# A planned two-layer kernel (cross attention, then a recurrent layer) on one core: one-bank matmul tiles are allotted to whichever step can begin, under a new table of due times

## Chip, cores and metric

The kernel runs on one core of a Trainium2 chip. The metric is device time in microseconds (us), from the start of the program to its end, and less is better. A core has five engines, each with its own instruction queue that it works through in order: TensorE (PE in the profile; PEld is its weight load), VectorE (DVE), ScalarE (ACT), GpSimd (POOL) and SyncE (SP), which here issues the transfers (DMAs) between the chip's main memory and the on-chip memories. Matmul results land in PSUM, a memory of banks of 128 x 512 numbers in f32; all other on-chip data lie in SBUF.

## The reference

Input: `x` and a context `ctx`, each 32 sequences x 128 tokens x 512 numbers, and a mask. Two layers follow each other; everything is f32.

Layer 0 is cross attention with 32 query heads and 8 key heads of 16 numbers:

```
q = x @ Wq + bq;  k = ctx @ Wk + bk;  v = ctx @ Wv + bv
attn = softmax(q k^T / 4 + mask);  x1 = layernorm((attn v) @ Wo + bo + x) * gamma + beta
```

Layer 1 is a recurrent layer with 32 heads of 16 x 16 state, whose start state comes from `ctx`:

```
xn = ln(x1);  sx = (xn of the token before) - xn
xxx = tanh((xn + sx*maa_x) @ maa_w1) -> five mixes;   x5[i] = xn + sx*(maa_stack[i] + xxx[i] @ maa_w2[i])
w = exp(-exp(time_decay + tanh(x5[1] @ decay_w1) @ decay_w2))
k = x5[0] @ Wk^T;  v = x5[2] @ Wv^T;  r = x5[3] @ Wr^T;  g = silu(x5[4] @ Wg^T)
per token t:  a = k_t v_t^T;  out_t = r_t (u*a + s);  s = a + w_t * s
x2 = x1 + (groupnorm(out) * g) @ Wo^T
xn2 = ln(x2);  xk, xr = xn2 + sx2 * (maa_k, maa_r)
y = x2 + sigmoid(xr @ fWr^T) * (relu(xk @ fWk^T)^2 @ fWv^T)
```

## The kernel before

**Work.** Both layers take the sequences in 16 pairs (`gr`, 256 tokens). Layer 0 (`attend`, L483) runs over all pairs first and leaves its result in main memory (`x1d`). Layer 1 is made of three functions for a pair:

- `front` (L998): the norm of a pair's rows `xt`, transposes on PE (`pxnt`), the shift (`sxt`) and the first mix (`xx`); `ph0` and a tanh give `h0`; `px5` (L1025) are small row-tiled matmuls whose results DVE turns into the five x5 (L1041: index 0 feeds k, 1 the decay, 2 v, 3 r, 4 g), to which POOL adds xn (L1055). Then `pdd` (L1090, column-tiled), and the big matmuls `pk`, `pv`, `pr`, `pg` (L938), each in two blocks (its first and second half of the channels, `_0` and `_2`) of eight matmuls, which the profile records as sixteen; `pew` gives the decay `ew`. v goes to main memory (`vd`, L1105).
- `recurrence` (L1180): four chunks `c` of 128 channels, and in each four values `dd`. v comes back spread over the partitions (`kv`, L1230, 1 MB in eight DMAs for two values of `dd`); ACT puts the start state into its first column (L1243), POOL multiplies it by k (L1252), DVE runs the recurrence as a scan (`a`, L1267) and multiplies by r (`ar`, L1281), and PE sums over the state (`acc`, L1296, column-tiled). `pd`, `own` and `pc` are the term of the token itself and the centring of the norm. `w4` (L1191) is the decay that the scan reads, one buffer.
- `tail` (L1336): `pvar` and `rstd` (an ACT square root, a DVE reciprocal), spread over heads by `pb` (L1357), the gate `gt`, `pwo` (L956), the sum `x1c` on DVE with its norm statistics, transposes `pxnc`, mixes `yk` and `yr`, then `pkk` (L938), `prr`, `pkv` (L956) and the result `rr`. The weights `fk` and `fr` come from main memory for each pair, into one buffer.

**Order.** No scheduler of the compiler decides the order. The kernel's own planner does, a class `Plan` (L152). `add` (L176) records a step: its engine, an assumed duration (`mm`, `dve`, `act`, `pool_`, L299 on), what it reads and writes, and a due time, which is the pair's number plus the entry of the table (`WHEN0` for layer 0, `WHEN1` for layer 1) under the step's engine and name. `give_out` (L238) then walks through an assumed run: on each engine it looks among the steps whose inputs are given out and which are due no more than `ahead` pairs after the earliest step left (SP's are free of that limit), takes the one that can begin soonest or, among those that begin within 0.3 us, the one that is due first, and emits the engine's instruction. So the table and the rule set the order in which instructions stand in each queue, and nothing else; waits between engines come from what is read and written.

**Places.** Tiles come from pools of a fixed number of buffers (`tag`, L168). In PSUM, layer 1 has one `a` (two banks), one `acc` (one bank), `w4` (two banks) and three buffers `g` of one bank each, which hold the result of every other matmul. In SBUF, `kv` has three buffers, `x5` four. `_turns` (L224) numbers the tiles of each tag by due time, and `_places` (L197) gives a step its place: it refuses if a tile's turn hasn't come, and if no buffer is free it takes the one whose last use ends first in the assumed run. The line on turns is the one that is changed:

```python
        if self.turns and any(c.turn - self.begun[c.tag] >= taken[c.tag] for c in fresh):
            return None, gone
```

Layer 0 has `turns` switched off (L425) and its own planner object.

Of the kernel before, what the change touches and what calls it, by code (L numbers as in the profile page):

```python
# [66 lines left out]
}  # L67
WHEN1 = {
    "ACT": """
        att 0: 8.9413, att 1: 10.3245, att 2: 10.9514, att 3: 4.2202, ew 0: 3.0530, ew 1: 7.1294, ew 2: 5.4799,  # L70
        ew 3: -0.1804, gt 0: 2.7896, gt 2: 7.2564, h0: 4.2793, hd: -0.7228, kk 0: 1.5652, kk 2: 8.9401,
        kv 0 0 0: 2.8237, kv 0 0 1: 2.8350, kv 0 1 0: 6.5988, kv 0 1 1: 4.7931, kv 1 0 0: 11.5248, kv 1 0 1: 12.1370,
        kv 1 1 0: 8.1713, kv 1 1 1: 8.4770, kv 2 0 0: 11.3074, kv 2 0 1: 0.7816, kv 2 1 0: 10.6862, kv 2 1 1: 7.1872,
        kv 3 0 0: 19.3264, kv 3 0 1: 5.1004, kv 3 1 0: 5.3317, kv 3 1 1: 6.5296, pk 0: 7.8527, pk 2: 3.7734,
        pv 0: 2.8655, pv 2: 13.4147, r 0: 10.0348, r 2: -0.1824, rr 0: 13.0999, rr 1: 2.8864, rstd: 5.6019,
        sq 0: -0.0986, sq 1: 8.8327, sq 2: 0.5974, sq 3: 5.6588, w4 0: 6.7771, w4 1: 3.1835, w4 2: 6.2518,
        w4 3: 1.3276, xnc 0: 5.1909, xnc 1: 3.5402, xnc 2: 5.5512, xnc 3: 9.4093, xnt 0: 4.3436, xnt 1: 6.3722,
        xnt 2: 7.1367, xnt 3: 8.6670, xx 0: 11.9355, xx 1: 6.5413, xx 2: 5.6875, xx 3: 9.8818, yk 0: 11.1356,
        yk 1: 1.7804, yk 2: 15.8112, yk 3: 13.9956, yr 0: 7.4657, yr 1: 8.8095, yr 2: 3.2938, yr 3: 8.7878,
        zc 0: 7.6581, zc 1: 0.9023, zt 0: 10.9657, zt 1: 5.2637  # L80
    """,
    "DVE": """
        a 0 0: -0.5883, a 0 1: -0.2414, a 0 2: 0.1043, a 0 3: 8.0118, a 1 0: 7.0047, a 1 1: 12.1762, a 1 2: 5.6912,
        a 1 3: 9.0685, a 2 0: 9.3322, a 2 1: 6.5083, a 2 2: 6.9110, a 2 3: 0.9712, a 3 0: 7.3177, a 3 1: 7.6874,
        a 3 2: 2.3097, a 3 3: 12.5406, ar 0 0: 2.4656, ar 0 1: 9.7666, ar 0 2: 5.7906, ar 0 3: 7.9178, ar 1 0: 6.6300,
        ar 1 1: 1.2202, ar 1 2: 6.5895, ar 1 3: 8.7855, ar 2 0: 28.3612, ar 2 1: 16.5392, ar 2 2: 12.3754,
        ar 2 3: 11.7973, ar 3 0: 9.1129, ar 3 1: 12.3189, ar 3 2: 9.0665, ar 3 3: 1.8400, gn 0: 8.4672, gn 1: 5.8193,
        gn 2: 3.6790, gn 3: 6.5194, gt 0: 0.0430, gt 2: -0.3529, own 0: 7.8602, own 1: 10.0300, own 2: 6.6987,
        own 3: 5.2960, pb 0: 0.7953, pb 1: 8.4093, pb 2: 4.1923, pb 3: 8.8563, raw 0: 2.2489, raw 1: 0.4033,
        raw 2: 5.9725, raw 3: 6.8204, rk 0: -0.4021, rk 1: 1.1444, rr 0: 7.1091, rr 1: 5.2378, rstd: 2.3485,  # L90
        st c 0: 6.9368, st c 1: 1.2521, st t 0: 8.7646, st t 1: 7.8543, x1c 0: 1.0294, x1c 1: 6.6954, x5 0 0: 2.9930,
        x5 0 1: 7.2539, x5 0 2: -1.0976, x5 0 3: 11.6924, x5 1 0: 8.4707, x5 1 1: -0.2943, x5 1 2: 10.2532,
        x5 1 3: 6.3221, x5 2 0: -0.6575, x5 2 1: 6.4713, x5 2 2: 12.8297, x5 2 3: 15.9903, x5 3 0: 6.5967,
        x5 3 1: 6.3600, x5 3 2: -0.8402, x5 3 3: -0.6696, x5 4 0: 8.4589, x5 4 1: 12.8956, x5 4 2: -0.4045,
        x5 4 3: 5.3981
    """,
    "PE": """
        acc 0: 13.3710, acc 1: 6.5427, acc 2: 6.5657, acc 3: 5.8187, pb 0: 18.0159, pb 2: 13.4697, pc 0: 0.6934,
        pc 1: 3.6234, pc 2: 5.2455, pc 3: 6.5762, pd 0: 1.0255, pd 1: 5.0703, pd 2: 6.9998, pd 3: 6.9286, pdd: 8.4674,
        pew 0: 6.2963, pew 2: 8.3876, pg 0: 1.2658, pg 2: 11.7555, ph0: 5.5651, pk 0: -0.5984, pk 2: -0.5853,  # L100
        pkk 0: 6.0318, pkk 2: 6.3700, pkv 0: 3.8400, pkv 1: 1.5996, pr 0: 0.4302, pr 2: -0.2452, prr 0: 3.2418,
        prr 1: 6.5661, pv 0: 20.6763, pv 2: -0.4713, pvar: 9.0706, pwo 0: 6.3422, pwo 1: 7.2520, px5 1 0: 6.5332,
        px5 1 2: 4.1685, px5 2 0: 10.0966, px5 2 2: 2.9044, px5 4 0: 2.5948, pxnc 0: 11.8548, pxnc 2: 5.6357,
        pxnt 0: 6.9871, pxnt 2: 5.3933
    """,
    "POOL": """
        kv 0 0 0: 5.5169, kv 0 0 1: 7.8442, kv 0 1 0: 9.0891, kv 0 1 1: 15.0789, kv 1 0 0: 17.4626, kv 1 0 1: 18.1051,
        kv 1 1 0: 6.4738, kv 1 1 1: 2.9970, kv 2 0 0: 11.4247, kv 2 0 1: 9.0041, kv 2 1 0: 5.1827, kv 2 1 1: 4.0282,
        kv 3 0 0: 7.8783, kv 3 0 1: 7.3985, kv 3 1 0: 8.4451, kv 3 1 1: 4.8441, rr 0: 5.3640, rr 1: 1.7889,
        sd c 0: 6.4756, sd c 1: 7.8170, sd t 0: 3.5686, sd t 1: 15.8010, sxc 0: 1.3067, sxc 2: 1.2094, sxt 0: 14.0948,  # L110
        sxt 2: 3.1827, x5 0 0: 6.6556, x5 0 2: 3.8406, x5 1 0: -0.9487, x5 1 2: 5.0243, x5 2 0: 7.7721,
        x5 2 2: 5.1770, x5 3 0: 5.2660, x5 3 2: 5.0072, x5 4 0: 17.6798, x5 4 2: 9.4950, xx 0: 0.3524, xx 2: 3.0003,
        yk 0: 7.2907, yk 2: 13.2242, yr 0: 7.8715, yr 2: 13.9395
    """,
    "SP": """
        fk: 4.3606, fr: 6.4556, kv 0 0 0: 17.3353, kv 0 1 0: 0.8314, kv 1 0 0: 11.4633, kv 1 1 0: 5.2653,
        kv 2 0 0: 13.6957, kv 2 1 0: 2.0768, kv 3 0 0: 0.9291, kv 3 1 0: 16.9878, rr 0: 1.7956, rr 1: 8.0232,
        s0 0: 0.8911, s0 1: 7.1710, vd 0: 4.3598, vd 1: 6.6057, vd 2: 0.4074, vd 3: 6.7184, x1c 0: 3.0367,
        x1c 1: 7.8990, x1t 0: 13.2705, x1t 1: 6.6624
    """,  # L120
}

# [29 lines left out]
class Plan:  # L152

    AFTER = {"PE": 0.25, "DVE": 0.1, "ACT": 0.15, "POOL": 0.12, "SP": 0.0}

    def __init__(self, ctx, tc, when, ahead):
# [38 lines left out]
    def _places(self, s):  # L197


        at, gone, taken = 0.0, [], {}  # L200
        fresh = [c for c in s.fresh if c.t is None]
        for c in fresh:
            taken[c.tag] = taken.get(c.tag, 0) + 1
        if self.turns and any(c.turn - self.begun[c.tag] >= taken[c.tag] for c in fresh):
            return None, gone
        taken = {}
        for c in fresh:
            pool, bufs, live = self.pools[c.tag]
            taken[c.tag] = taken.get(c.tag, 0) + 1
            if len(live) + taken[c.tag] <= bufs:  # L210
                continue
            best = None
            for o in live:
                if o not in gone and all(u.end is not None for _, _, u in o.uses):
                    end = max(u.end for _, _, u in o.uses)
                    if best is None or end < best[0]:
                        best = (end, o)
            if best is None:
                return None, gone
            at = max(at, best[0] + 0.1)  # L220
            gone.append(best[1])
        return at, gone
# [15 lines left out]
    def give_out(self):  # L238
        self.turns and self._turns()
        left = {id(s): len(s.before) for s in self.steps}  # L240
        ready = {e: [] for e in self.AFTER}
        free = {e: 0.0 for e in self.AFTER}
        for s in self.steps:
# [4 lines left out]
        while todo:  # L248
# [3 lines left out]
            for e, ss in ready.items():  # L252
                pick = None
                for s in ss:
# [3 lines left out]
                    for s0 in s.before:  # L258
                        at = max(at, s0.end + (0.0 if s0.eng == e else self.AFTER[s0.eng]))
                    room, _ = self._places(s)  # L260
# [68 lines left out]
def xattn_rwkv_kernel(  # L329
# [53 lines left out]
    x1c = [Cell(None, None, f"x1d_{b}", t=x1d[b]) for b in range(B)]  # L383
# [37 lines left out]
    with ExitStack() as sa:  # L421
        wa = sa.enter_context(tc.tile_pool(name="wa", bufs=1))
        wt = sa.enter_context(tc.tile_pool(name="wt", bufs=3))
        pl = Plan(sa, tc, WHEN0, 15.2739)
# [30 lines left out]
        for i in range(2):  # L455
            t = wa.tile([T, G, 4, 2, 2, S], F32, name=f"v2_{i}")
# [5 lines left out]
        for i in range(4):  # L462
            t = dram.tile([4, 8, T], F32, name=f"rd_{i}")
            rds.append(Cell(None, None, f"rd_{i}", t=t))

        for c in range(KC):
# [13 lines left out]
                r=[pt],  # L480
# [326 lines left out]

    pl = Plan(ctx, tc, WHEN1, 13.2672)  # L810
    fix = ctx.enter_context(tc.tile_pool(name="fix", bufs=1))
    for tag, bufs in (("xt", 2), ("xc", 2), ("s0", 3), ("z", 3), ("xn", 2), ("sx", 2), ("x5", 4), ("h0", 1), ("hd", 1)):
        pl.tag(tag, bufs)
# [11 lines left out]
    kx, vx, vd = [], [], []  # L825
    for i in range(2):
        t = fix.tile([P, KC, G, T], F32, name=f"kx{i}")
        kx.append(Cell(None, None, f"kx{i}", t=t))
        t = fix.tile([P, KC, 1 + N], F32, name=f"vx{i}")
# [3 lines left out]
        for c in range(KC):  # L833
            t = dram.tile([HC, 4, 4, N], F32, name=f"vd{i}_{c}")
# [3 lines left out]
    t = wp.tile([P, 4, G, T], F32, name="w4")  # L838
    for i in range(2):
        nc.vector.memset(t[:, 2 * i : 2 * i + 2], 0.0)  # L840
    w4 = Cell(None, None, "w4", t=t)
# [683 lines left out]
```

## Time and profile before

| | us |
|---|---|
| three runs | 2156.69, 2154.84, 2150.53 (median 2154.84) |
| the profiled execution by its own clock | 2150.95 |
| its span, first to last instruction | 2149.2 |
| PE busy in the span (a weight load beside it: 1305.8) | 1992.6 (93%) |
| DVE / POOL / ACT busy | 1783.0 (83%) / 1294.0 (60%) / 1058.0 (49%) |
| mean clock granted to TensorE | 0.962 |
| first layer-1 load (`x1t`) / first `acc` / last `acc` begin at | 633.7 / 695.8 / 2088.9 |
| moved by DMA | 252.23 MB, mean 117 GB/s |

How to read it: the profile comes from one execution, with every engine's instructions on one time axis. "Busy" is the time in which an engine had an instruction in work; matmuls overlap each other, so a busy PE is not PE at its peak. "Idle before" is the gap ahead of an instruction, with the instruction or DMA that ended it. The granted clock is the share of its full speed at which TensorE was let run. In lines, `px` stands for `px5`, `x` for `x5`, `w` for `w4` and so on: trailing numbers of names are left out.

The costliest single groups of layer 1 are the 256 products on POOL (`kv`, 2349 ns each), the 256 scans on DVE (`a`, 2294 ns) with their 256 products (`ar`, 1217 ns), and on PE the blocks of L938 and L956, about 120 us in all for each of `pk`, `pv`, `pr`, `pg`, `pkk`, `pwo`, `pkv` and `prr`.

### The profile page before, as it was taken

To read this page: it belongs to the slowest core of one execution; us is meant where nothing else is said; L and a number is where in the kernel's file an instruction comes from. 1 tells how busy PE (TensorE), PEld (TensorE's weight loads), DVE (VectorE), ACT (ScalarE), POOL (GpSimd) and SP (SyncE) were. 2 spreads that over 40 slices of the span, in tenths; PEclk is the share of its full clock that TensorE was granted. 3 is DMA by queue.
4 is the path that set the end of the run, shared out by engine and by line. 5 is a ranking of instruction groups with operands and counts; after the bars stand their busy time and mean duration, and the time that the engine had idled before them with its cause. 6 is when DMAs were issued, how large, how long until landed. Compare 5 with 4: busy or idle time off the path is not lost.

```text
span 2149.2 us, 36169 instructions
## 1 busy us (share of the span) xinstructions
PE 1992.6 (93%) x11908; PEld 1305.8 (61%) x11908; DVE 1783.0 (83%) x2182; ACT 1058.0 (49%) x3473; POOL 1294.0 (60%) x1081
## 2 busy tenths in 40 slices
PE   5999999999958779999999999999999999999977
PEld 4666666666626546566675665656657566575643
DVE  3888888888844888989988899898988989888881
ACT  3888888888842233433434434344343443433332
POOL 1273334343345666777777777777777877777552
PEclk9999999999978889999999999999999999999988
DMA  7232221221024687887977978879788797886851
GB/s 207 61 127 66 62 70 60 68 61 60 27 81 80 114 121 114 146 158 122 175 122 138 167 117 168 130 138 163 120 161 134 141 165 117 162 136 115 163 99 59
DMA packets 155883, 252.23 MB, mean 117 GB/s; under 512 B 50512, under 2 KB 97648, under 8 KB 139312
## 3 DMA queue, kind: packets, MB, share of 16 engines
q1 hardware_dynamic: 149232, 240.27, 59.8%
q10 hardware_dynamic: 6464, 9.66, 1.4%
q8 instruction: 94, 1.54, 0.4%
q14 instruction: 93, 0.76, 0.1%
HBM read 224.12 MB, written 25.69 MB: 116 GB/s over the span
## 4 chain that ended last, share of the span: by engine, by line
PE 52%; DVE 7%; ACT 2%; DMA 1%; issue 1%; POOL 0%; SPq 0%; POOLq 0%; DVEq 0%; ACTq 0%
PE pkk L938 5%; PE pwo L956 5%; PE pk L938 5%; PE pv L938 5%; PE pr L938 4%; PE acc L1296 4%; PE pkv L956 4%; PE pg L938 4%; PE prr L956 4%; DVE a L1267 3%; PE pdd L1090 2%; PE px L1025 2%; DVE x L1041 2%; PE pc L1321 1%; PE pew L1162 1%
## 5 line engine op out<-in xcount | busy, mean ns | idle before, releaser
L1252 POOL TENSOR_TENSOR kv<-kv,kx 128x1016 f32<-128x1016 f32 x256 | 597.6, 2349 | 142.9 <-DMA kv<-vd 63.1
L1267 DVE TENSOR_TENSOR_SCAN a<-w,kv 128x1024 f32<-128x1024 f32 x256 | 587.3, 2294 | 29.1 <-ACT w L1191 8.0
L653 ACT ACTIVATE pr<-pr,mx 128x128 f32<-128x128 f32 x1024 | 398.3, 391 | 53.4 <-DVE mx L641 47.0
L1281 DVE TENSOR_TENSOR ar<-a,r 128x1024 f32<-128x1024 f32 x256 | 311.5, 1217 | 4.4
L1055 POOL TENSOR_TENSOR x<-x,xnt 128x512 f32<-128x512 f32 x160 | 187.2, 1181 | 92.1 <-DVE x L1041 79.4
L653 ACT ACTIVATION_READ_ACCUMULATOR pr<-pr,mx 128x1 f32 x1024 | 193.7, 189 | 0.0
L1041 DVE SCALAR_TENSOR_TENSOR x<-px,col,sxt 128x256 f32<-128x256 f32 x320 | 133.9, 473 | 59.5 <-PE pdd L1090 37.2
L629 DVE TENSOR_TENSOR pr<-sc,m 128x1024 f32<-128x1024 f32 x128 | 153.7, 1210 | 32.1 <-PE sc L613 29.0
L665 PE MATMUL ppT<-ident,pr 128*128 128x128 f32 x1024 | 154.3, 281 | 12.1 <-DVE pT L672 4.3
L665 PEld LDWEIGHTS ppT<-ident,pr 128*128 128x128 f32 x1024 | 115.4, 141 | 77.9 <-issue 25.9
L641 DVE TENSOR_REDUCE mx<-pr 128x8 f32<-128x1024 f32 x128 | 155.5, 1215 | 2.7
L1296 PE MATMUL acc<-ar,give 128*32 128x256 f32 x2048 | 142.5, 394 | 12.6 <-DVE ar L1281 12.6
L672 DVE COPY pT<-ppT 128x512 f32<-128x512 f32 x192 | 128.3, 682 | 22.9 <-PE ppT L665 18.2
L397 POOL TENSOR_SCALAR sd_a<-mv_a 128x1 f32<-128x1 f32 x32 | 7.1, 223 | 214.6 <-DVE mv_a L393 214.5
L716 PE MATMUL pw<-wo,oT 128*128 128x512 f32 x256 | 122.3, 610 | 9.8 <-POOL oT L711 8.8
L938 PE MATMUL pkk<-yk,fk 128*128 128x256 f32 x512 | 121.4, 392 | 6.2 <-POOL yk L905 6.2
L956 PE MATMUL pwo<-wo,gt 128*128 128x512 f32 x256 | 122.2, 612 | 5.0 <-ACT xnt L868 2.9
L938 PE MATMUL pr<-x,wr 128*128 128x256 f32 x512 | 122.0, 387 | 3.8 <-DVE x L1041 3.8
L557 PE MATMUL pq<-xT,wq 128*128 128x256 f32 x512 | 122.9, 389 | 0.7 <-ACT xT L512 0.7
L938 PE MATMUL pk<-x,wk 128*128 128x256 f32 x512 | 123.3, 390 | 0.0
L956 PE MATMUL pkv<-fv,kk 128*128 128x512 f32 x256 | 120.3, 603 | 0.0
L938 PE MATMUL pg<-x,wg 128*128 128x256 f32 x512 | 117.6, 383 | 2.9 <-DVE x L1041 2.9
(146 smaller groups left out, 3714.7 us busy)
## 6 DMA issues: line engine op xcount, KB each, us to landing
kv<-vd SPq DMA_DIRECT2D x1024, 128.0 KB
fk<-in_fWkT_dram SPq DMA_DIRECT2D x16, 1024.0 KB
fr<-in_fWrT_dram SPq DMA_DIRECT2D x16, 1024.0 KB
x<-in_x_dram SPq DMA_DIRECT2D x32, 256.0 KB
ct<-in_ctxT_dram SPq DMA_DIRECT2D x32, 256.0 KB
bc<-rd SPq DMA_DIRECT2D x256, 32.0 KB
x1d<-z SPq DMA_DIRECT2D x32, 256.0 KB
x1t<-x1d SPq DMA_DIRECT2D x32, 256.0 KB
```

Source lines behind the costliest of these rows:

```text
L629: lambda b=b, sc=sc, jp=jp, pr=pr: nc.vector.tensor_tensor(pr(), sc()[:, 2 * jp : 2 * jp + 2].rearrange("p j g e s -> p (j g e) s"), ms[b] ...
L641: lambda pr=pr, mx=mx: nc.vector.tensor_reduce(mx(), pr(), AX.X, ALU.max, negate=True),
L653: nc.scalar.activation(pr()[:, 4 * i + h, :], pr()[:, 4 * i + h, :], AF.Exp, bias=mx()[:, 4 * i + h : 4 * i + h + 1], accum_out=sm()[:, h0 ...
L665: nc.tensor.transpose(pt()[:, h, :], pr()[:, 4 * i + h, :], ident)
L938: nc.tensor.matmul(pp()[:, i], (w() if isinstance(w, Cell) else w)[:, kc, (c + i) * P : (c + i + 1) * P], flat(src()[:, kc]), start=(kc == 0),
L956: nc.tensor.matmul(pp(), src()[:, c, b, :], (w() if isinstance(w, Cell) else w)[:, c, :], start=(c == 0), stop=(c == KC - 1),)
L1041: lambda i=i, c=c, pp=pp, half=half: nc.vector.scalar_tensor_tensor(flat(ts[i]()[:, c]), pp()[:, half], col[:, MS0 + i, c : c + 1], flat(s ...
L1055: lambda i=i, c2=c2: nc.gpsimd.tensor_add(ts[i]()[:, c2 : c2 + 2].rearrange("p c b t -> p (c b) t"), ts[i]()[:, c2 : c2 + 2].rearrange("p ...
L1252: lambda c=c, kv=kv, e=e: nc.gpsimd.tensor_tensor(kv()[:, e, :, :, 1:T], kv()[:, e, :, :, 1:T], k()[:, c, :, 0 : T - 1].unsqueeze(1).broad ...
L1267: lambda kv=kv, a=a, e=e: nc.vector.tensor_tensor_scan(a().rearrange("p j b t -> p (j b t)"), w4().rearrange("p j b t -> p (j b t)"), kv() ...
L1281: lambda c=c, a=a, ar=ar: nc.vector.tensor_tensor(ar(), a().rearrange("p j b t -> p j (b t)"), flat(r()[:, c]).unsqueeze(1).broadcast_to([ ...
L1296: nc.tensor.matmul(acc()[32 * j : 32 * j + 32, :N], give[:, d].rearrange("p e h -> p (e h)"), tiles[d]()[:, j], start=(d == 0), stop=(d == 3),
```

## The change

A new class attribute names a tag, `g`, whose tiles have no turns: a step that needs one may take a free buffer as soon as it can begin, whatever is due earlier. All other tags keep their turns. The table `WHEN1` is another one, found by a search under this rule (its entries now reach up to 45 pairs, so that many steps are ordered by what depends on them, since a step is due no later than what follows from it), and `ahead` of layer 1 goes from 13.2672 to 3.9465. Layer 0, the steps themselves, their assumed durations and the number of buffers stay.

```diff
@@ class Plan
+    FREE = ("g",)
     AFTER = {"PE": 0.25, "DVE": 0.1, "ACT": 0.15, "POOL": 0.12, "SP": 0.0}
@@ def _places(self, s):
-        if self.turns and any(c.turn - self.begun[c.tag] >= taken[c.tag] for c in fresh):
+        if self.turns and any(c.tag not in self.FREE and c.turn - self.begun[c.tag] >= taken[c.tag] for c in fresh):
             return None, gone
@@ layer 1
-    pl = Plan(ctx, tc, WHEN1, 13.2672)
+    pl = Plan(ctx, tc, WHEN1, 3.9465)
@@ WHEN1, "PE"
-        acc 0: 13.3710, acc 1: 6.5427, acc 2: 6.5657, acc 3: 5.8187, pb 0: 18.0159, pb 2: 13.4697, pc 0: 0.6934,
...
+        acc 0: 11.6056, acc 1: 19.5265, acc 2: 29.4448, acc 3: 27.8814, pb 0: 8.7430, pb 2: 16.8465, pc 0: 3.6989,
...
```

## The prediction

> **What bounds the kernel now.** First the page's span in 40 slices. Each slice is 53.7 us; the attention layer fills the first eleven, the recurrent layer the rest.
>
> ```profile
> PE   5999999999958779999999999999999999999977
> DVE  3888888888844888989988899898988989888881
> PEclk9999999999978889999999999999999999999988
> ```
>
> From slice 16 to 38 PE is busy throughout and VectorE (DVE) nearly so. The attention layer isn't touched, so only what comes after about 633 us counts. The chain of work that ended last names PE in nearly every piece there, and its pieces repeat: one pair of sequences ("a period") after the other. I cut the recurrent layer at that repeat and asked for busy time by stretch (stretch, length, then busy us and count of PE, weight load, DVE, ACT, POOL, then clock, DMA share, GB/s):
>
> ```profile
> 891.00:978.14 87.14, 84.69 (x473) 55.41 (x473) 79.31 (x90) 35.03 (x77) 65.89 (x51) 1.00 0.83 148
> 978.14:1066.70 88.56, 86.11 (x473) 55.89 (x473) 79.29 (x90) 35.06 (x77) 65.85 (x51) 0.98 0.83 144
> 1066.70:1155.35 88.65, 86.20 (x473) 55.87 (x473) 79.29 (x90) 35.17 (x77) 65.86 (x51) 0.98 0.84 143
> 1865.27:1957.93 92.66, 88.06 (x476) 56.72 (x476) 83.28 (x95) 36.12 (x78) 70.57 (x55) 0.98 0.80 137
> ```
>
> A period is 88.7 us (ten of the twelve I cut lie at 88.6 to 89.1). One, at full clock, is 1.5 us shorter with the same work; one is 4 us longer. DVE alone needs 79.3 us, the DMA engines 0.83 of the time. So PE bounds, and DVE is 9 us behind it.
>
> Where PE isn't working shows in its timeline of one period (start, length, operation; in brackets the wait before it):
>
> ```profile
> 987.22 1.33 PE L1025 MATMUL px<-h,w 32*128 32x256 f32 x8
> 988.47 0.66 PE L860 MATMUL pxnc<-ident,zc 128*128 128x128 f32 x4
> 991.26 0.64 PE L1090 MATMUL pdd<-x,wd 128*32 128x256 f32 x2 [2.13 <-DVE x L1041]
> ...
> 996.13 1.13 PE L1025 MATMUL px<-h,w 32*128 32x256 f32 x8
> ...
> 1053.86 0.70 PE L1357 MATMUL pb<-rstd,back 32*128 32x256 f32 x4
> ...
> 1057.57 1.44 PE L1357 MATMUL pb<-rstd,back 32*128 32x256 f32 x4
> 1059.23 1.98 PE L956 MATMUL pwo<-wo,gt 128*128 128x512 f32 x4 [0.22 <-ACT xnt L868]
> ```
>
> PE waits 2.13 us for DVE's x5 before `pdd`, and the 32 `pdd` matmuls then take 3.4 us. In the one period at clock 1.00 they take 1.9, behind the same wait:
>
> ```profile
> 904.12 0.41 PE L1090 MATMUL pdd<-x,wd 128*32 128x256 f32 x2 [2.13 <-DVE x L1041]
> ```
>
> Record lengths 0.41 against 0.64 us: after this wait the clock drops in 12 of the 13 periods from 891 us on. Beside it, four `pb` take 1.44 us once and 0.70 elsewhere, eight `px` 1.33 and 1.13, and `pwo` waits 0.22: 1.2 us more of waits. So a period is 88.7 - 2.1 - 1.5 - 1.2 = **83.9 us of PE work**.
>
> [...]
>
> **The change, part by part.** No instruction is added or removed; only the order on each engine differs, which the built programs show.
>
> *Wait before `pdd`.* New order on PE: `px5` of x5 1 and 0, half a `pwo`, two `pd`, eight matmuls `pk` (which need x5 0), then `pdd`. x5 0 is now first on DVE and on POOL. Behind the second `px` stand on DVE four x5 (1.6 us) and on POOL one add (1.18), beside 1.7 + 0.9 us of `pwo` and `pd` on PE; x5 1 comes one POOL add later, beside 3.45 us of `pk`. So -2.1, and with it the drop, -1.5. If that cover failed, what comes late is `pk`, by up to the 2.1 again.
>
> *Waits at `pb` and `pwo`.* The four `pb` now stand apart, the transposes `pxnt` far ahead: -1.2. Bounds: 0 to -1.2.
>
> *More changes of matmul kind.* PE's order has 30 changes per period between full-array, row-tiled, column-tiled and transposing matmuls before, 34 after; returns to full array 9 before, 14 after, entries to row tiling 8 and 7. The price is in the chain:
>
> ```profile
> 1009.51 1.00 PE acc L1296 x16
> 1010.51 3.65 PE pv L938 x16
> 1014.16 3.45 PE pkk L938 x16
> ```
>
> Sixteen matmuls take 0.20 us more behind a tiled group. Net 4 x 0.20 = **+0.8** (bounds 0 and 1.2). [...]
>
> *New waits.* Three slots of the one-bank tag now hold what could begin, and some are given back late. From the end of the second `pwo` to the start of the second `pkk`, the latter takes the slot that DVE's first two x5 of index 3 free; the built program has it wait for DVE. DVE's way there starts with the `x1c` of that same `pwo`. Its prices, from the timeline:
>
> ```profile
> 1000.46 2.29 DVE L1267 TENSOR_TENSOR_SCAN a<-w,kv 128x1024 f32<-128x1024 f32 x1
> 1002.78 1.22 DVE L1281 TENSOR_TENSOR ar<-a,r 128x1024 f32<-128x1024 f32 x1
> 1004.09 2.30 DVE L1267 TENSOR_TENSOR_SCAN a<-w,kv 128x1024 f32<-128x1024 f32 x1
> ```
>
> A scan with its product takes 3.65 us start to start. On DVE: five such pairs 18.25, one more product 1.2, `x1c` with its statistics 1.9, five `own` 2.05, one gate 0.6, four x5 1.6: 25.6 us. On PE between the same points: `pd` twice 0.9, `pk` 3.45, `pdd` 1.9, eight transposes 1.15, `pc` 0.6, `acc` 1.0, `pg` 3.65, `px` 1.05, `pkk` 3.65, `acc` 1.0, `pd` 0.6, `pk`, `pc`, `pk` 3.9: 22.85. So PE waits 25.6 - 22.9 = **+2.7**, in two or three pieces (the first `pkk` waits for the gate, the second `pk` for x5 index 2). Bounds: 0, if DVE enters the stretch ahead, and 2.7 + 1.5, if the last piece drops the clock. A wait of 1.31 us late in this trace was followed by matmuls at full speed, 2.13 us by slow ones; the last piece is about 1.4 to 1.8, so I take no drop.
>
> *DMA.* The stores of v and the fetches of kv behind them (SP, in order) move: the second `pv` is now the last matmul block of a period, its stores pass behind two fetches. They issue some 6 us into the next period and their data is multiplied on POOL some 28 us into it, and a fetch takes 10 to 12 us (below), so 0. Bounds 0 and +1, the rest is the slower rival.
>
> *Sum of a period.* 83.9 + 0.8 + 2.7 = 87.4 against 88.7: -1.3, times the 14 periods between the first and the last pair: **-18 us**.
>
> *Start.* `pv` of pair 0, whose stores open the first scan, stands behind both `pk` and four transposes instead of one `pk`: +3.65 + 0.6, less about 1 that DVE saves later: +3 (0 to +6). *End.* The last `prr` waited 1.74 us for its weights; now all of `pkv` (3.4 us more) stands ahead of it: -2 (0 to -4).
>
> Sum against the profiled execution, 2150.95 us by its own clock (span 2149.2 and 1.8 around it): 2150.95 - 18 + 3 - 2 = **2134 us**. The runs shown have the median 2154.84, 0.2% above that execution; less than 0.3% (6.5 us) can't be told from no change here.
>
> **The rivals.**
>
> *The new wait isn't there.* If DVE reaches the stretch with 2.7 us in hand, a period is 84.7 and the time 2150.95 - 14 x 4.0 + 1 = 2096. For it: DVE has 79.3 us of work in 84.7. Against it: its stretch begins with a result of PE that is nowhere else made up.
>
> *The wait comes in one piece, and the clock drops.* 87.4 + 1.5 = 88.9: 2150.95 + 3 + 1 = 2155, no change. For it: 2.13 us does it in 12 of 13. That the new order isn't built, which would give the same, is excluded: all five engines' orders differ.
>
> *The fetches bind (slower).* A kv buffer is free at the end of a scan; then eight issues, the landing, two copies on ACT (0.3) ahead of the relu (0.6) that frees the slot of the next `pd` (0.6). On DVE 13.5 us lie between that scan and the `own` that needs this `pd`. From the timelines of SP and ACT, fetches issued at 1002.88 in 3.54 us were there at 1012.89 (10.0), those issued at 1110.13 in 5.20 at 1122.44 (12.3). 13.5 - 1.5 = 12.0: from there each further us is a us per period, and PE then stands long enough for the drop. At 13.5 us: 87.4 + 1.5 + 1.5 = 90.4, 2150.95 + 24 + 1 = 2176. For it: the 92.66 us period is such a case (its chain has three kv landings of 2.7 to 8.3 us). Against: the fetches at issue here start with an empty queue, as those of 10.0 did.
>
> **How the numbers follow.** Forecast (2120 to 2144) 0.45; no new wait 0.15; clock drop 0.20; fetches 0.20. Faster is the first two, 0.60; same 0.20; slower 0.20. The predicted time is the forecast's, 2134, its own range 2120 to 2144. The wide range reaches down to the second case (2096) and up into the slower one (2172), leaving out about half of each.
>
> **What would show it.** Stretches of 87.4 us at clock 1.00; `pdd` in 1.9 us with no wait; waits for DVE at `pkk`, 2 to 3 us together; sixteen-matmul blocks of 3.65 us more often. Clock 0.98 means the second rival; DVE or PE waiting for kv, or ACT's kv copies waiting with PE idle behind them, the third. The prediction fails if a place that I haven't followed (start, three slots elsewhere in the period) costs more than 1 us per period.

## The result and the profile after

| | before | changed |
|---|---|---|
| median of 8 runs (us) | 2156.53 (2150.53 to 2159.85) | 2146.35 (2143.84 to 2148.52) |
| ratio, 95% interval | | 0.9955 (0.9943 to 0.9966) |
| profiled execution, its span | 2150.95, 2149.2 | 2148.52, 2146.7 |

The changed kernel is 0.45% faster. The forecast was 2134 us; its own range (2120 to 2144) ends 2.4 us below the median. The sign was right; the gain forecast, 17 us from its base, was 1.7 times the 10.2 of the medians and four times what the traced executions show (below).

The page's slices of the changed kernel look as before; the clock row differs by a tenth in three of them, and 53.7 us is too coarse to say why:

```profile
PE   5999999999958789999999999999999999999986
DVE  3788888888852799988898898999988998999881
PEclk9999999999988789999999999999999999999998
```

Busy time by stretch, cut from one `pvar` (it runs once per pair) to the next; four periods of the changed kernel, columns as in the prediction:

```profile
1313.51:1403.01 89.50, 86.80 (x473) 55.11 (x472) 79.80 (x90) 34.35 (x77) 65.88 (x51) 0.98 0.80 147
1403.01:1490.88 87.87, 85.16 (x473) 54.58 (x473) 79.82 (x90) 34.36 (x77) 65.94 (x51) 1.00 0.79 141
1490.88:1578.74 87.86, 85.16 (x474) 54.58 (x473) 79.81 (x90) 34.41 (x77) 65.97 (x51) 1.00 0.81 145
1578.74:1666.60 87.86, 85.16 (x473) 54.57 (x473) 79.80 (x90) 34.40 (x77) 65.92 (x51) 1.00 0.82 145
```

A period is 87.86 us at clock 1.00 (forecast 87.4), against 87.14 in the one such period of before. **At full clock the changed kernel is 0.72 us per period slower.** What it wins is clock: 3 of its 13 steady periods are 1.64 us longer (first line), against 12 of 13 before. The timeline of PE in the period that starts at 1490.88:

```profile
1521.06 0.41 PE L1092 MATMUL pdd<-x,wd 128*32 128x256 f32 x2
...
1531.19 3.69 PE L940 MATMUL pkk<-yk,fk 128*128 128x256 f32 x16 [1.03 <-issue]
1534.81 1.07 PE L1298 MATMUL acc<-ar,give 128*32 128x256 f32 x16
1535.82 0.70 PE L1209 MATMUL pd<-rk,share 128*128 128x256 f32 x2
1536.80 1.99 PE L940 MATMUL pk<-x,wk 128*128 128x256 f32 x8 [0.29 <-DVE x L1043]
...
1541.92 1.99 PE L940 MATMUL pkk<-yk,fk 128*128 128x256 f32 x8 [0.97 <-DVE x L1043]
```

`pdd` runs at full speed (0.41) without a wait. PE waits at `pkk` and `pk` instead: with 0.24 at `pb` and 0.16 at `px`, 2.69 us per period, no piece over 1.03. "issue" names nothing; the instruction there waits for DVE's gate (`gt`), which ended 0.1 us earlier.

Two profiled executions of each kernel, cut at `pvar` of pairs 1, 13 and 15 (us):

| | before | before, again | changed | changed, again | forecast of the difference |
|---|---|---|---|---|---|
| start to pair 1 | 871.2 | 872.0 | 870.6 | 870.1 | +3 |
| 12 periods | 1063.0 | 1063.0 | 1059.6 | 1057.8 | -15.6 |
| the next two | 158.1 | 158.5 | 160.8 | 161.8 | -2.6 |
| to the end | 56.8 | 56.7 | 55.7 | 54.8 | -2 |

By their means the changed kernel is 1.3 + 4.3 - 3.0 + 1.5, or about 4, us faster, not the medians' 10.2: both traced executions of before (2150.95 and 2152.15) are among its fastest. In 32 of its executions beside the experiments (2151 to 2165 us), 0.001 less of mean granted clock goes with 1.4 us more (correlation -0.88). That points to the clock here too, but no trace shows where those slower executions lost it.

### The profile page after: what moved, and what is told of

Read it like the earlier page. It is cut to its first block, busy times and chain, and to the rows that moved or that the text cites. A ratio compares the mean times of both kernels' runs of the same rounds, so it can differ in the third digit from the quotient of the medians.

```text
span 2146.7 us, 36138 instructions
## 1 busy us (share of the span) xinstructions
PE 1988.3 (93%) x11908; PEld 1291.2 (60%) x11908; DVE 1791.6 (83%) x2182; ACT 1046.3 (49%) x3473; POOL 1295.2 (60%) x1081
## 5 line engine op out<-in xcount | busy, mean ns | idle before, releaser
L1438 POOL TENSOR_TENSOR rr<-rr,x1c 128x512 f32<-128x512 f32 x32 | 40.6, 1269 | 166.1 <-DVE rr L1434 162.1
L958 PE MATMUL pwo<-wo,gt 128*128 128x512 f32 x256 | 130.0, 636 | 2.4 <-DVE gt L1374 2.4
L940 PEld LDWEIGHTS pkk<-yk,fk 128*128 128x128 f32 x512 | 95.8, 194 | 58.9 <-issue 23.0
L958 PE MATMUL prr<-fr,yr 128*128 128x512 f32 x256 | 122.9, 606 | 2.4 <-DVE rr L1434 1.7
```

What stands on the lines that cost most here:

```text
L940: nc.tensor.matmul(pp()[:, i], (w() if isinstance(w, Cell) else w)[:, kc, (c + i) * P : (c + i + 1) * P], flat(src()[:, kc]), start=(kc == 0),
L958: nc.tensor.matmul(pp(), src()[:, c, b, :], (w() if isinstance(w, Cell) else w)[:, c, :], start=(c == 0), stop=(c == KC - 1),)
```

## The experiments

**What was asked.** Why does the clock drop, and why does a period take 0.46 us more than forecast? A scan of the granted clock in slices of 0.1 us shows each drop as 3.4 us (or a multiple) at 0.50. In the trace of before they begin at

```
990.7  1079.5  1168.2  1257.0  1345.7  1434.5  1523.2  1612.0  1700.7  1789.5  1878.2  1956.7  1970.4
```

that is 88.75 us apart from 990.7 to 1878.2. Steps of the length of a drop that fit 26 times into that are 887.5 / 260 = 3.413 us long; 1956.7 to 1970.4 is 4 x 3.413. Its periods run 87.14, 88.56, 88.65, 88.70, 88.72, 88.74, 88.74, 88.74 (then 88.90 and again 88.67, 88.71, 88.73): they converge on that number. In the changed kernel drops begin at 978.7, 1156.2 and 1333.7, 52 x 3.413 apart, and in the 3.4 us before each of them PE's longest wait is 0.16 us. Hence two theories. A matmul on 128 rows (`128*128` or `128*32` in the profile's lines) is called full-height here, the column-tiled ones included; a row-tiled one is on 32 or 64 (`32*128`, `64*128`). **W**, the forecast's: a wait of about 2 us drops the clock, shorter ones don't. **G**: drops begin on a grid of these 3.413 us that lies elsewhere in each execution, and a step of the grid with too little matmul work in it is followed by one at clock 0.50. For the waits: the forecast's **chain** (DVE's queue is behind, one debt in three pieces) against separate **loops (L)**.

**How single instructions were moved.** The planner's walk records its order, listed moves are made in one engine's queue, then the instructions are emitted; with an empty list the program is the same as before. This shifts line numbers in those profiles. e1 to e6 and e9 are one execution each, so what they show is read from periods and waits in the trace rather than from the total.

```diff
-            s.fn()
+            order.append((s, new, wait_for))
@@ at the end of give_out
+        self._emit(order)
```

A move reads: direction, engine, step, which of its parts, the step it goes to, pairs between the two, that step's part, pairs. Rule and table can't be had singly: old table under the new rule, or new table under the old one, and the walk ends with steps that all wait for places, also with other values of `ahead`. `ahead` itself moves nothing: either table gives the same program with 13.2672 and 3.9465.

**e1, the kernel before, again** (no edit).

> The kernel before, unchanged, for a second profile. Theory W (the forecast's): a wait of 2.13 us ahead of pdd drops the clock because it is long; drops then begin 0 to 0.5 us behind the start of that wait, at any time on the axis, and the period is 88.7 because 87.14 + 1.6 is. Theory G (grid): the clock is set anew every 3.413 us on a fixed grid, half speed for one such step when the step before it held too little matmul work; drops then begin at whole multiples of 3.413 us from each other, wherever they lie in the kernel, last 3.41 or a multiple of it and cost 1.71 us of full-speed time each, and the period of 88.73 us is a lock at 26 steps (26 x 3.413 = 88.75). G expects one drop per period in this execution too, and the times of executions to differ by the number of drops outside the locked periods (first 180 and last 100 us of the layer).

2152.15 us. Drops in 11 of the 12 periods from pair 1 to 13, beginning at 906.1, 994.9, 1083.6, 1172.4, 1261.1, then none, then 1435.2 (1261.1 + 51 x 3.413) and on every 88.7. The place where it slips shows the bound. Two steps of this execution and the step behind each:

```profile
1346.50:1349.90 3.40, 1.34 (x28) 1.02 (x32) 3.04 (x4) 2.21 (x5) 2.89 (x3) 1.00 0.45 87
1349.92:1353.32 3.40, 3.40 (x41) 1.85 (x34) 2.73 (x3) 2.23 (x6) 2.13 (x3) 1.00 1.12 142
1257.76:1261.10 3.34, 1.24 (x24) 0.97 (x28) 3.08 (x4) 2.24 (x5) 2.83 (x3) 1.00 0.38 88
1261.15:1264.55 3.40, 3.40 (x32) 1.54 (x24) 2.21 (x3) 1.59 (x4) 1.19 (x2) 0.50 1.15 142
```

The wait of 2.13 us lies in both first lines; with 1.34 us of PE work beside it the next step has clock 1.00, with 1.24 (1.32 over the step's full 3.41 us) it has 0.50. W fell: the wait is the same. G stands, and in these steps the bound lies low in that range: the step from 902.0 in the trace of before, in its one period without a drop, holds 1.33 us.

```profile
902.04:905.45 3.41, 1.33 (x26) 1.01 (x30) 3.06 (x4) 2.24 (x5) 2.90 (x3) 1.00 0.42 87
905.45:908.85 3.40, 3.40 (x41) 1.86 (x34) 2.70 (x3) 2.21 (x5) 2.12 (x3) 1.00 1.08 145
```

**e2, before, two DVE instructions moved** (x5 of index 3 ahead of a scan).

```diff
+    ("ahead", "DVE", "x5 3 2", 0, "a 1 3", -1, 0, range(3, 14)),
+    ("ahead", "DVE", "x5 3 3", 0, "a 1 3", -1, 0, range(3, 14)),
```

> The kernel before, with one pair of DVE instructions moved in pairs 3 to 13: the two x5 of index 3 (from the second px5 of index 2), whose slot pdd waits for, go ahead of the scan that stood before them. Both theories: the 2.13 us wait before pdd falls to 0.3 to 0.6 us. Theory W: with it the drop goes, the period is 88.7 - 1.7 - 1.6 = 85.3 to 85.6 us. Theory G: the same if the step around px5 and pxnc now holds enough work (the px5 are row-tiled), and then the period is free of the lock at 26 steps; if not, drops stay in a part of the periods. Rival N (the next wait takes its place, DVE's scan being 0.5 us later): 87.1 at full clock.

2130.93 us, 24 less than the run of before beside it, on the old table. A period, and its `pdd`:

```profile
1303.94:1390.29 86.35, 85.14 (x473) 55.23 (x472) 79.30 (x90) 34.84 (x78) 66.27 (x51) 1.00 0.84 149
```

```profile
1335.16 0.41 PE L1163 MATMUL pdd<-x,wd 128*32 128x256 f32 x2 [0.47 <-DVE x L1114]
```

The wait fell by 1.66 and the drop went (none from 819 to 1856 us); of the 1.66, 0.87 came back, most of it at `acc`, which now waits 0.28 for DVE and takes 0.42 more. Between the expected 85.4 and rival N.

**e3, changed, an `acc` block between `px5` and `pew`.**

```diff
+    ("ahead", "PE", "acc 0", 1, "pew 2", 0, 0, range(3, 14)),
```

> The changed kernel, with one acc block (16 matmuls, 1.0 us) moved on PE from behind pew to between px5 and pew, pairs 3 to 13; all waits stay as they are. In the changed kernel 3 of 13 periods hold a drop, each behind px5 and pew (row-tiled) with no wait of over 0.2 us near; the drop was there when a grid step began within 0.12 us of one place in the period. Theory G: a step that held px5, pew and 0.35 us of acc was just under the bound; with the acc between them every step holds 1 us of acc, so no drop at all in the steady periods: all at 87.86. Theory W has no reason for these drops and expects no change: about 3 of 13 at 89.5.

No drop from 796 to 2024 us; the eleven periods from pair 2 to 13 are 87.85 to 87.87, the ones on either side 88.05 and 88.08; 2140.44 us. What it had removed, in the trace of the changed kernel (a step and the next):

```profile
1152.80:1156.20 3.40, 3.24 (x21) 1.89 (x24) 3.19 (x9) 0.23 (x1) 1.02 (x4) 1.00 0.33 80
1156.25:1159.65 3.40, 3.40 (x19) 1.39 (x8) 2.36 (x2) 1.46 (x5) 2.23 (x2) 0.50 0.79 156
```

PE was busy for 3.24 of 3.40 us and the clock still fell: 1.75 us were `px5` on 32 of 128 rows, 1.06 `pew` on 64, and only 0.44 full-height. Busy time alone doesn't tell these steps apart: 1.34 us of it had no drop behind it in e1. W, with every wait left in place, expected no change.

**e4, changed, one DVE product ahead of four x5.**

```diff
+    ("ahead", "DVE", "ar 1 0", 0, "x5 0 2", 1, 0, range(3, 14)),
```

> The changed kernel, with one DVE product (ar of chunk 1, first value, 1.22 us) moved ahead of the four x5 for which DVE waited 1.34 us (for px5), so that the wait is filled and everything behind on DVE is 1.2 us earlier; pairs 3 to 13. The forecast's chain (DVE from x1c to the x5 of index 3 sets all of PE's three waits, 1.03 + 0.29 + 0.97): the sum of the waits falls by 1.2, the last of them first, period 87.86 - 1.2 = 86.65. Rival L: the last wait (0.97, second pkk) is not DVE's queue but a loop of its own: the x5 of index 3 takes the buffer that the pk just ahead on PE has read; then the first two fall (1.03 to 0, 0.29 to about 0.1) and the 0.97 stays: also 86.65, but told apart by which wait is left. Rival N: the period stays, another wait grows.

87.23 at full clock, -0.63, half of what both expected; 2140.86 us. (Five of 13 periods held a drop, three of them in a row at 88.87, 26.04 steps.) PE's waits in its timeline:

```profile
1521.81 3.69 PE L1012 MATMUL pkk<-yk,fk 128*128 128x256 f32 x16 [0.39 <-issue]
...
1527.42 1.99 PE L1012 MATMUL pk<-x,wk 128*128 128x256 f32 x8 [0.29 <-DVE x L1115]
...
1532.54 1.99 PE L1012 MATMUL pkk<-yk,fk 128*128 128x256 f32 x8 [0.97 <-DVE x L1115]
```

Only the first wait moved; the last, which the chain names as the first to shrink, stayed to the hundredth. So 0.64 of the first wait was DVE's queue being behind, as the chain has it. The rest is a loop: DVE now waits 0.59 for ACT, which reads the `pg` that PE has just ended.

**e5, the changed kernel, again** (no edit).

> The changed kernel, unchanged, for a second profile. Theory G (the clock is set in steps of 3.413 us on a grid that lies elsewhere in each execution): full-clock periods are 87.86 us again (25.74 steps, so that the place of the grid in the period moves by a quarter of a step each time), and a drop falls in 0 to 5 of the 13 steady periods, always behind px5 and pew, at a different set of pairs than in the first profile. Theory W expects the same periods to be slow as in the first. From the start to the second pvar: the first profile had 870.6 us, two kernels with the same start had 865.4 and 865.8; expected here 865 to 871.

2146.34 us. Drops at 1592.9, 1770.4 and 1947.9 (again 52 steps apart) in place of 978.7, 1156.2 and 1333.7; the other periods 87.86 to 88.06. Other pairs are slow in another execution: G.

**e6, changed, an `acc` block into the wait before the second `pkk`.**

```diff
+    ("ahead", "PE", "acc 2", 0, "pkk 2", -1, 0, range(3, 14)),
```

> The changed kernel, with the first acc block of chunk 2 (16 matmuls, 1.0 us) moved on PE ahead of the second pkk, pairs 3 to 13, so that it stands where PE waits 0.97 us. Loop theory L (the wait before the second pkk is the way of PE's own pk through the buffer of x5 to DVE's x5 of index 3 and back): the 0.97 goes to nothing, period 87.86 - 0.97 = 86.9, the other two waits (1.03, 0.29) unchanged. The forecast's chain (all waits are DVE being behind): the wait only moves, DVE being no faster, and the first pkk of the next period or the pk waits 1 us more: 87.86.

86.86, -1.00; 2132.23 us. That the 0.97 is gone and nothing else changed shows in PE's waits, summed over nine periods (950 to 1750 us): total, times, longest. First the changed kernel (its three longest totals), then e6:

```profile
PE pkk L940 <- issue: 9.3, 9, 1.0
PE pkk L940 <- DVE x L1043: 8.7, 9, 1.0
PE pk L940 <- DVE x L1043: 2.6, 9, 0.3
```

```profile
PE pkk L1012 <- issue: 9.3, 9, 1.0
PE pk L1012 <- DVE x L1115: 2.6, 9, 0.3
PE pb L1431 <- DVE gt L1226: 2.4, 10, 0.2
PE px L1099 <- DVE x1c L1460: 1.4, 9, 0.2
```

The chain fell: were DVE behind as a whole, a block moved on PE would have won nothing. The wait is a local one, as L says: `pkk` needs the slot that the x5 of index 3 frees. What that x5 waits for is less settled. In the changed kernel two things end as it begins, on PE and on DVE:

```profile
1539.06 1.89 PE L940 MATMUL pk<-x,wk 128*128 128x256 f32 x8
1539.78 1.23 DVE L1283 TENSOR_TENSOR ar<-a,r 128x1024 f32<-128x1024 f32 x1
1540.99 0.88 DVE L1043 SCALAR_TENSOR_TENSOR x<-px,col,sxt 128x256 f32<-128x256 f32 x2
```

One is the `pk` whose input buffer the x5 takes over, which is L's loop; the other is a scan and a product on DVE. Both paths start at the x5 of index 2, and their ends lie within 0.06 us of each other. So these runs don't show which of the two sets the 0.97; this x5 moved ahead of that scan, as in e2, would show it and wasn't run.

**e7, changed, the moves of e3, e4 and e6 together.**

> The changed kernel with three moves together, pairs 3 to 13: ar ahead of the four x5 (alone 87.23 at full clock), acc of chunk 2 ahead of the second pkk, acc of chunk 0 between px5 and pew (alone no drop). If the three are separate, 87.86 - 0.64 - 0.97 = 86.25 us with no drop, 11 periods: about 2146 - 11 x 1.6 - 3 x 1.6 = 2123 to 2126. If DVE is the bound behind them, 86.9 to 87.2: 2133.

86.23 in eleven periods, no drop; median 2120.20 us, ratio to before 0.9841 (0.9815 to 0.9868). The three are separate, and this beats both kernels:

```profile
1471.51:1557.74 86.23, 85.13 (x473) 54.58 (x473) 79.93 (x90) 34.34 (x77) 65.85 (x51) 1.00 0.82 148
```

**e8, before, the moves of e2 in all pairs and an `acc` behind `pxnt`.**

```diff
+    ("behind", "PE", "acc 0", 1, "pxnt 2", 1, 0, range(1, 15)),
```

> The kernel before with two moves, all pairs where they exist: the two x5 of index 3 ahead of a scan (in pairs 3 to 13 alone: 86.35 us at full clock, no drop), and on PE the second acc block of chunk 0 from ahead of the transposes pxnt to behind them, where four pb took 1.44 instead of 0.70 us and pwo then waited 0.22, both for ACT's copies of those transposes. If the acc fills that wait: 86.35 - 0.96 = 85.4 us, and 2131 - 13 x 0.95 - 2 x 2 = 2114 to 2120. If DVE (79.3 us of work, with its own waits) takes over, 86.0 to 86.35 and 2126 to 2131. The old table with two moves is then 1 to 1.5% ahead of the changed kernel.

86.15 and 2127.14 us (ratio 0.9862, 0.9843 to 0.9882), -0.20 instead of -0.96: the waits at `pb` and `pwo` went, but the transposes, without the `acc` ahead of them, wait for a slot from DVE:

```profile
1481.52 1.06 PE L934 MATMUL pxnt<-ident,zt 128*128 128x128 f32 x8 [0.61 <-DVE gt L1446]
```

A one-bank slot's way back took the place of the wait removed.

**e9, e7 with four `pb` out of a `pv` block.**

```diff
+    ("behind", "PE", "pb 0", 0, "pv 2", 1, -1, range(3, 14)),
```

> The changed kernel with the three moves of the run before (full-clock period 86.23) and a fourth, pairs 3 to 13: the first four pb (row-tiled), which stand alone between the two halves of a pv block, go behind the second half, next to acc and the other pb. That takes away one entry to row tiling and one return to full array, and the wait of 0.24 us ahead of them. The forecast's price (0.20 us per change and return): 86.23 - 0.24 - 0.20 = 85.8 us. Price nothing: 86.0. Rival: the gate that DVE makes of these pb comes later than the first pwo needs it, a wait of its own of up to 2 us: 86.2 or more.

86.24, no change; 2121.77 us. From start to next start, less the waits, `pv` takes 7.01 in place of 7.26 per period: **0.25 us is the price of one break of a full-array block**, measured on this one. But as much came back: the second `pb` take 0.99 instead of 0.70, and `ph` starts 0.23 later behind the first `pwo`, both without a wait that the profile names. That DVE returns the slots of the moved `pb` later would explain it, a kin of the rival; it wasn't tried.

**e10, e7's moves in more pairs** (`range(1, 15)` or `(2, 15)`).

> The changed kernel with the three moves in all pairs where they can stand (1 or 2 to 14, in place of 3 to 13). Two or three more periods 1.6 us shorter: 2120 - 3 to 5 = 2115 to 2117, if the periods at the edges are set by the same waits; 2120 if they are set by something else (transfers at the end of the last pairs).

2125.06 us (2117.30 to 2132.26), ratio 0.9849 (0.9826 to 0.9871): no gain over e7. In its traced execution the periods at the edges are shorter (86.42 and 85.83 for 88.07 and 88.13), but pair 1 comes at 876.3 in place of 866.1. A drop of two grid steps stands there, from 834.3 us, that e7's trace doesn't have; what else delays the first pairs wasn't followed.

**e11 and e12, before with useless matmuls.**

```diff
             def turn(c2=c2, pt=pt):
+                if which == "c" and c2 == 2:
+                    for k in range(3):
+                        nc.tensor.matmul(flat(pt()[:, 0]), w2[:, 0:P], w2[:, 0:N], start=True, stop=True)
```

In e12 the operands are `w2[0:32, 0:P]` and `w2[0:32, 0:N]`.

> The kernel before with useless work added in every pair: three full-array matmuls (six records, 1.29 us) of constants, put on PE ahead of the second pxnc transposes, that is into PE's wait before pdd; the transposes write over their result, nothing reads it. Nothing is taken away or moved. All theories: PE's wait falls from 2.13 to about 0.85 us and the full-clock period stays 87.14. Theory W (the length of the wait) and G (too little work in a grid step; the step now holds 1.3 us more of full-array work, over the 1.31 to 1.36 us at which steps of the profiles so far parted) both: no drop, 87.1 in all steady periods, so 11 or 12 x 1.6 = 18 us less: 2138, ahead of the changed kernel's 2146. If drops have nothing to do with PE's work: 2156.

> The same useless three matmuls in the same place, but on 32 of the 128 rows (row-tiled, as px5), which take PE as long. Theory W (only the time in which PE stands counts: 0.85 us): no drop, 87.1 us a period, 2138. Theory G, by which row-tiled work counts for a quarter or less: the step around px5, the useless matmuls and the wait holds about 0.6 us from them and 0.66 of transposes, under the bound: the drop stays in most periods, 88.7, 2156.

e11: **2136.79 us, ratio 0.9899 (0.9883 to 0.9914). e12: 2155.85 us, ratio 0.9993 (0.9979 to 1.0007).** A period of e11, then one of e12:

```profile
1304.90:1392.04 87.14, 86.05 (x480) 56.56 (x479) 79.31 (x90) 34.97 (x78) 66.05 (x51) 1.00 0.86 147
```

```profile
1392.40:1481.14 88.74, 87.52 (x480) 56.95 (x479) 79.36 (x91) 34.82 (x77) 65.90 (x51) 0.98 0.85 143
```

The timelines at the useless matmuls and behind them, e11 and then e12:

```profile
1336.35 1.56 PE L860 MATMUL pxnc<-w 128*128 128x256 f32 x6
1337.75 0.60 PE L863 MATMUL pxnc<-ident,zc 128*128 128x128 f32 x4
1339.14 0.41 PE L1093 MATMUL pdd<-x,wd 128*32 128x256 f32 x2 [0.78 <-DVE x L1044]
```

```profile
1433.77 1.56 PE L861 MATMUL pxnc<-w 32*128 32x256 f32 x6
1435.26 0.66 PE L864 MATMUL pxnc<-ident,zc 128*128 128x128 f32 x4
1436.83 0.64 PE L1094 MATMUL pdd<-x,wd 128*32 128x256 f32 x2 [0.91 <-DVE x L1045]
```

Same count, same length, same place, and about the same wait left: with 128 rows `pdd` runs at 0.41, with 32 rows at 0.64. In e12 the step before a drop shows PE busy for 2.82 us:

```profile
1433.10:1436.50 3.40, 2.82 (x18) 2.03 (x16) 3.40 (x5) 1.09 (x4) 2.24 (x2) 1.00 0.00 0
1436.55:1439.95 3.40, 3.12 (x32) 1.57 (x32) 1.26 (x2) 1.54 (x4) 2.90 (x2) 0.51 0.91 157
```

W is out: the wait is 0.91 us there. Work that nobody needs takes 1.0% off the old kernel, more than the whole change does.

## Why the prediction was wrong, step by step

- **Wait before `pdd`, -2.1: right** (2.13 to 0).
- **"and with it the drop, -1.5": this is the step whose mechanism failed.** The size per drop was right (1.6 us), the cause wrong. I took the wait's length for it ("2.13 us does it in 12 of 13", "the last piece is about 1.4 to 1.8, so I take no drop"). e3, e11 and e12 show that a grid step with little full-height work does it: with the wait at 0.8 to 0.9 us the drops went in e11 and stayed in e12. In the changed kernel drops remained in 3 of 13 periods, behind `px5` and `pew`, where I saw nothing to price. Over the 12 periods of the table the clock gave 1.1 us per period, not 1.5. The second rival ("in one piece, and the clock drops") had the right thing left over for the wrong reason.
- **Waits at `pb`, `px`, `pwo`, -1.2: half.** `pb` -0.74 and `pwo` -0.22 came; `px` grew by 0.55, most of it in one group that is held up behind its first two matmuls.
- **Changes of matmul kind, +0.8: too small.** "Net 4 x 0.20" counted all changes against each other. `pg`, `pkk`, `pwo`, `pd`, `pr`, `pv` and `pk` together take 1.5 more. e9 prices one full-array block broken by tiled matmuls at 0.25, so this is six breaks' worth; that all of it is breaks was not tried. The transposes and `pc`, which I hadn't followed, take 0.86 less.
- **New waits, +2.7: 2.69, right by its sum only, and that is luck.** It wasn't one debt of 25.6 us of DVE against 22.85 of PE. 0.64 of it was DVE's queue (e4); 0.97 was a local wait that a block of that length filled whole (e6), though DVE did no less; the 0.29 before the second `pk` moved in neither.
- **Sum of a period.** At full clock +0.26 was forecast and +0.72 measured; with the clock -1.3, and -0.36 measured (4.3 over 12). Of the 0.9 that is missing, 0.4 is the clock and 0.5 the waits and changes of kind above.
- **"times the 14 periods".** The last two belong to the drain: +3.0 in place of -2.6 (the one into pair 14 is 3 to 4 us shorter, the one into pair 15 6 to 7 longer; its chain stands at fetches of kv, which the slower rival had looked for in every pair). **Start** -1.3 for +3, **end** -1.5 for -2.
- **DMA in steady periods, 0: right.** DVE waits 1.3 us in all for kv between 800 and 1900 us.
- **The base.** The sum stood on one execution of before that was one of its fastest; from the median, 2156.53, the same 17 us less would have been about 2140.

In the traces of before and of the changed kernel every drop, those outside the steady periods too, begins within 0.1 us of one grid of 3.413 us per trace. What marks a step that is followed by a drop is less plain than a wait: one with 1.32 us of work was followed by one (e1), and so was one with 3.24 us of mostly row-tiled work (the changed kernel, from 1152.8).

## What to carry to other kernels

Before a gain is put down to a wait, cut the granted clock finely: here the drops, which lie on a grid of 3.41 us, came from too little full-height matmul work in one step, not from the wait's length, and a period that with its drop makes a whole number of steps (88.74 us, 26 of them) paid for one in 12 of 13 turns. Then look at what stands around row-tiled matmuls; here one full block between them took the three drops away (e3), and useless work (e11) won 1.0%, more than the new schedule's 0.45%. And a wait for a slot can be local, with the engine that gives it back not behind as a whole: a ready block of the same length filled one of 0.97 us whole here (e6), where earlier work on the neighbour had left it as it was (e4).

## What the runs showed of the hardware

- **The loop of before ran in step with the drops' grid.** 87.14 us of work became 88.74, 26 steps of 3.413 us; the periods approach 88.75 from below (88.56 to 88.74). I read it so: a drop at the same place in each turn brings the next turn to the same place. The changed kernel's 87.86 us (25.74 steps) didn't lock, and its drops came 52 steps, two periods, apart.
- **What counted as work.** Idle with column-tiled work beside it: 1.32 us in a step was too little (e1), 1.33 enough (before). With 2.65 to 2.80 us of row-tiled work: 0.44 to 0.48 us of full-height work beside it was too little (the changed kernel's steps from 975.3, 1152.8 and 1330.3), 0.60 and 0.61 enough (from 1507.8 and 1770.6), each matmul counted from its start to the next one's. Both fit one bound of 1.33 if the row-tiled time counts for 0.28, (1.33 - 0.60) / 2.65, to 0.31, (1.33 - 0.48) / 2.78, of itself, an estimate from these steps. The bound doesn't fit everywhere, and how 32 and 64 rows differ stays open: near the end of e3 (from 2021.4) a step with 1.24 us of full-height and 0.70 of row-tiled work was followed by a drop, and late in the trace of before one with 1.48 us of transposes, `pd` and `acc`:

```profile
2052.33:2055.74 3.41, 1.48 (x14) 0.62 (x12) 3.27 (x3) 1.94 (x4) 2.04 (x2) 1.00 0.42 53
2055.74:2059.16 3.42, 1.08 (x8) 0.20 (x8) 2.05 (x4) 2.83 (x7) 2.08 (x2) 0.50 0.93 156
```

- **The run-to-run spread** of the kernel before (2151 to 2165 us) follows the mean granted clock (0.965 to 0.955), as it would if each execution meets the grid elsewhere; that last is not shown.
